# Scoring part of the edges of a graph attention layer with edges on partitions

## The chip, the cores and the metric

The kernel runs on one core of one Trainium2 chip. The metric is the device time of one execution in microseconds (us); the figure given is the median of several runs. The engines named here are TensorE (PE in the profile; its weight loads are shown as PEld), VectorE (DVE), ScalarE (ACT), GpSimd (POOL) and the queue that issues the transfers (SP).

## The reference, cut to what matters

Four graph layers, each with a layer norm and a relu ahead of it and a residual sum behind it, work on x of shape 128 x 64 x 256 (batches, nodes, features). The change touches the fourth layer only, a graph attention with 4 heads of 64 features over 512 edges. Its input H is the normed x; A0 is the adjacency matrix; src and dst are the two ends of each edge.

```python
Xq = (H @ W_lin.T).reshape(bt, n, h, dh)
Xv = (H @ W_val.T).reshape(bt, n, h, dh)
Qs = Xq[:, src]
Kt = Xq[:, dst]
e = jnp.einsum('behd,hd->beh', jax.nn.leaky_relu(Qs + Kt, LRELU_SLOPE), a)
e = e + jnp.log(A0[src, dst] + EPS)[None, :, None]
e_t = e.transpose(1, 0, 2)
m = jax.ops.segment_max(e_t, src, num_segments=n)
ex = jnp.exp(e_t - m[src])
denom = jax.ops.segment_sum(ex, src, num_segments=n)
attn = ex / denom[src]
Vt = Xv[:, dst].transpose(1, 0, 2, 3)
Y = jax.ops.segment_sum(attn[..., None] * Vt, src, num_segments=n)
return Y @ W_out.T
```

LRELU_SLOPE is 0.2, so leaky_relu(z) is 0.2 z + 0.8 relu(z). The 0.2 part is linear in Xq and is formed per node; the 0.8 relu part has to be formed per edge. It is the second part that the change forms in another way.

## The kernel before, in words

All arithmetic is float32. Nearly all instructions are recorded under line 799 of the kernel, a helper which every operation goes through, so the profile is read by the names of tiles.

The fourth layer (`layer3`, from line 2416) works through 32 steps g = 0..31. A step holds 4 of the 128 batches. The 32 steps form 4 groups of 8 steps, and a group's scores are collected in one PSUM tile acc of 128 x 512: 32 batches x 4 heads on partitions, the 512 edges in columns. The steps of a group go through these functions:

- `turned` (line 2471, in even steps): the layer norm of the next block of 8 batches (tile h, pool with two slots), its transposes (h to ps, copied to hT) and the sums hS which the next function needs.
- `queries` (line 2501, in odd steps): seven products, from which Q (the Xq of 8 batches, nodes on partitions) and XV (their Xv) are put together by additions on VectorE. Then `linear` (2535): Q times 0.2 a (tile lin_p), reduced to lin by two reductions, the linear part of the score per node.
- `score` (2550): for each of two halves fc of the features and each of the 4 batches k, one matmul of 64 rows: weights are Q (64 nodes x 128 features), the moving operand is S2, which holds a one for each end of each edge (64 nodes x 512 edges). Even and odd k use partitions 0 to 63 and 64 to 127. The result ps (128 features x 512 edges) goes through a relu on ScalarE into r (8 slots). So a step has eight score matmuls and eight relus, ps with features on partitions.
- `reduce` (2563): eight matmuls add r into acc, with weights from apad, which holds 0.8 a in the columns of the step's batches and heads (64 columns wide; even k go to the upper, odd k to the lower half of acc). The first step of a group writes the logarithm of A0 into acc.
- `summed` (2643, at the end of a group): one matmul adds the linear part, lin times S2. Then `softmax` with `shifted` (2631, 2647): scans along the edges on VectorE over acc, the exponential on ScalarE; `edgewise` (2659), a group later: the transposes of the result into at.
- For step v = g - 10, ten steps behind: `between` (2671) multiplies at by the one-hot OST (tiles aw, 5 slots, four products of 128 x 1024 on VectorE per step) and gathers them by matmuls with ODT (ps, then an); `weighted` (2698) multiplies an with XV into y; `output` (2714) multiplies y with W_out, adds the result to X on VectorE and sends X to HBM.
- The first eight steps also bring back blocks of X that had been put aside (`back`, line 2227: transposes of ls_t into ps, added to X by VectorE).
- `turn` (2576) finishes the last group and the steps which are still open, in an order written out by hand.

The ps tiles of all these functions share five PSUM slots; acc and y have one place each. Outside `turn` the order on each engine is made when the kernel is built, from the order in the program and from when operands are expected to be ready; within an engine the instructions then stand in that order. So a function which stands late in the program can be placed into an earlier gap of its engine.

Of the kernel before, what the change touches and what calls it, by code (L numbers as in the profile page):

```python
# [8 lines left out]
F32 = mybir.dt.float32  # L9
I32 = mybir.dt.int32  # L10
AF = mybir.ActivationFunctionType
ALU = mybir.AluOpType
# [63 lines left out]
class Eig:  # L76
# [12 lines left out]
    def t(self, name, *shape, dt=F32):  # L89
        key = (name, shape)  # L90
        if key not in self.tiles:
            n = "e_" + name + "_" + "_".join(map(str, shape))
            self.tiles[key] = self.pool.tile([64, *shape], dt, name=n)
        return self.tiles[key]
# [748 lines left out]
class Plan:  # L843
# [56 lines left out]
    def rest(self):  # L900

        while any(self.queue.values()):
            for e in self.queue:
                self.fill(e, 1e9)
# [8 lines left out]
class Fast:  # L913
# [229 lines left out]
    def scale(self):  # L1143
# [32 lines left out]

        Q = t("Q", 64, 2, 64)
        o.ts(Q[:, 0, :], D[:], mid[:], ALU.subtract, sc[:], ALU.mult)
        nes = self.NE = t("NEs", 64, 64)
        o.ts(nes[:], NE[:], sc[:], ALU.mult)  # L1180
        o.stt(Q[:, 1, :], nes[:], -1.0, nes[:], ALU.mult, ALU.mult)
        self.ne2 = Q[:, 1, :]
        p = self.mm((self.k.ones[0:1, :], Q[0:1, :, :].rearrange("p a b -> p (a b)")), p=128, n=128)
        DD, E2 = self.DD, self.E2 = t("DD", 128, 64), self.ME[:, 1, :]
# [258 lines left out]
B, N, D = 128, 64, 256  # L1443
P = 128
NB = 16
TPB = 4
BT = 512
E = 512
HEADS = 4
# [16 lines left out]
class Kernel:  # L1466
# [949 lines left out]
    def layer3(self):  # L2416
        nc, o, io = self.nc, self.o, self.io
        cx, (w,) = self.stage([("l3x", 1)], "tile")
        with cx:
            cy, pools = self.stage([("l3", 2), ("l3v", 2), ("l3s", 1), ("l3r", 6), ("l3ps", 5), ("l3cps", 1), ("l3yps", 1)], "tile")  # L2420
            with cy:
                self.a02 = self.everywhere(w, "ed_a", io["L3_gnn_a"].rearrange("h d -> (h d)"))
                o.ts(self.a02[:], self.a02[:], 0.2, ALU.mult)
                self.drop, self.dropr = (w.tile([P, E], F32, name="ed_" + n) for n in ("drop", "dropr"))
                o.ts(self.drop[:], self.cont[:], 1.0, ALU.subtract, FLOOR, ALU.mult)
                o.ts(self.dropr[:], self.contr[:], 1.0, ALU.subtract, FLOOR, ALU.mult)
                WQV = w.tile([P, 2, 2 * D], F32, name="w3_qv")
                for x, n in enumerate(("W_lin", "W_val")):
                    nc.sync.dma_start(WQV[:, :, x * D:(x + 1) * D],
                                      io[f"L3_gnn_{n}_t"].rearrange("(k p) m -> p k m", p=P))  # L2430
                WO = self.weights(w, "w3_o", io["L3_gnn_W_out_t"])


                st, LAG = {}, 10
                self.turned(st, 0, *pools)
                WQV = self.sums3(w, WQV)
                self.queries(st, 0, WQV, *pools)()
                for g in range(8 * NG):
                    v = g - LAG
                    ahead = (g + 1) // 2 if g % 2 and g + 1 < 8 * NG else None  # L2440
                    self.score(st, g, *pools)
                    if v >= 1:
                        self.weighted(st, v - 1, *pools)
                    self.reduce(st, g, *pools)
                    if g % 8 == 1 and 1 < g:
                        self.edgewise(st, g // 8 - 1, *pools)
                    if v >= 0:
                        self.between(st, v, *pools)
                    if g % 8 == 7 and g + 1 < 8 * NG:
                        self.summed(st, g // 8, *pools)  # L2450
                    if g < 8:
                        self.back(8 + g, pools[4], "ps")
                    if ahead:
                        rest = self.queries(st, ahead, WQV, *pools)
                    elif g + 2 < 8 * NG:
                        self.turned(st, g // 2 + 1, *pools)
                    if g + 6 == 8 * NG:

                        p = pools[4].tile([P, BT], F32, name="ps")
                        for c in range(4):  # L2460
                            self.nc.tensor.transpose(p[:N, c * P:(c + 1) * P], self.OST[:, c, :], self.ident[:])
                        self.act_copy(self.cont[:N, :], p[:N, :])
                    if v >= 1 and g + 1 < 8 * NG:
                        self.output(st, v - 1, WO, *pools)
                    if ahead:
                        rest()
                    if g % 8 == 7 and g + 1 < 8 * NG:
                        self.softmax(st, g // 8, *pools)
                self.turn(st, WO, pools)
# [31 lines left out]
    def queries(self, st, i, WQV, pool, vp, sp, rp, psum, psc, psy):  # L2501

        nc, o, (A, S1, S2, S3) = self.nc, self.o, st["sums", i]
        Q = st["Q", i] = rp.tile([P, TPB, D], F32, name="Q", bufs=1)
        V = st["V", i] = rp.tile([P, TPB, D], F32, name="XV", bufs=7)
# [29 lines left out]
    def linear(self, st, i, pool, vp, sp, rp, psum, psc, psy):  # L2535

        o, Q = self.o, st["Q", i]

        if i % 4 == 0:
            st["lin", i // 4] = pool.tile([P, 2, 2, 8, HEADS], F32, name="lin")  # L2540
            self.nc.vector.memset(st["lin", i // 4][:], 0.0)
        lin, pr = st["lin", i // 4], sp.tile([P, TPB, D], F32, name="lin_p")
        o.mul(pr[:], Q[:], self.a02[:, None, :].to_broadcast([P, TPB, D]))
        k = 2 * (i % 4)
        for x in range(2):
            s = slice(64 * x, 64 * x + 64)
            o.red(lin[s, x, :, k:k + 2, :].rearrange("p m a h -> p a m h"),
                  pr[s].rearrange("p (a m) (h d) -> p a m h d", m=2, h=HEADS), ALU.add)

    def score(self, st, g, pool, vp, sp, rp, psum, psc, psy):  # L2550

        rs = st["r"] = []
        Q = st["Q", g // 2]
        for fc in range(2):
            for k in range(4):
                s = slice(64 * (k % 2), 64 * (k % 2) + 64)
                p = psum.tile([P, E], F32, name="ps")
                self.mm(p[:], Q[s, 2 * (g % 2) + k // 2, fc * P:(fc + 1) * P], self.S2[s, :])
                r = rp.tile([P, E], F32, name="r", bufs=8)
                self.act(r[:], p[:], AF.Relu)  # L2560
                rs.append(r)

    def reduce(self, st, g, pool, vp, sp, rp, psum, psc, psy):


        q, i = g // 8, g % 8
        if i == 0:
            st["acc", q] = psc.tile([P, E], F32, name="acc")
            self.mm(st["acc", q][:], self.ones[0:1, :], self.logA[:], True, False)
        for fc in range(2):  # L2570
            for k in range(4):
                z = 64 - 32 * (k // 2) - 4 * i
                x = 64 * (k % 2)
                self.mm(st["acc", q][x:x + 64, :], self.apad[:, fc, z:z + 64], st["r"][4 * fc + k][:], False, False)

    def turn(self, st, WO, pools):

# [64 lines left out]

    def summed(self, st, q, pool, vp, sp, rp, psum, psc, psy):

        self.mm(st["acc", q][:], st["lin", q][:].rearrange("p x m a h -> p (x m a h)"), self.S2[:], False, True)

    def shifted(self, st, q, pool, vp, sp, rp, psum, psc, psy):
# [144 lines left out]
```

## Time and profile before

| what | value |
| --- | --- |
| median of 3 runs | 2331.29 us (2325.34 to 2333.49) |
| the profiled execution | 2327.79 us |
| its span, from first to last instruction | 2326.0 us |
| fourth layer in that span | about 1746 to 2322.6 us |
| granted TensorE clock, mean | 0.997 |

Times in the profile are microseconds from the start of the span, unless marked ns. "out<-in" names the tiles that an instruction writes and reads; "128*64" behind a matmul is the part of the array it uses, rows by columns; "128x512" is partitions by elements; "x16" counts records, and one matmul call in float32 leaves two records, each with its weight load. The busy time of an engine counts stretches in which at least one of its instructions runs, so for matmuls that run beside each other it is less than count times mean. In a timeline the bracket behind an instruction is the time for which its engine had stood idle ahead of it, and what ended that.

### The profile page before, as it was taken

To read this page: it belongs to the slowest core of one execution; us is meant where nothing else is said; L and a number is where in the kernel's file an instruction comes from. 1 tells how busy PE (TensorE), PEld (TensorE's weight loads), DVE (VectorE), ACT (ScalarE), POOL (GpSimd) and SP (SyncE) were. 2 spreads that over 40 slices of the span, in tenths; PEclk is the share of its full clock that TensorE was granted. 3 is DMA by queue.
4 is the path that set the end of the run, shared out by engine and by line. 5 is a ranking of instruction groups with operands and counts; after the bars stand their busy time and mean duration, and the time that the engine had idled before them with its cause. 6 is when DMAs were issued, how large, how long until landed. Compare 5 with 4: busy or idle time off the path is not lost.

```text
span 2326.0 us, 33145 instructions
## 1 busy us (share of the span) xinstructions
PE 2283.2 (98%) x12365; PEld 1664.8 (72%) x12365; DVE 1642.2 (71%) x4073; ACT 1129.4 (49%) x2468; POOL 3.0 (0%) x26
## 2 busy tenths in 40 slices
PE   7999998999999999999999999999999999999999
PEld 4555446986777788888999998888885544554544
DVE  7887676998447777666766666559756686766667
ACT  5666864654436654443444444336435544444321
POOL 0000000000000000000000000000000000000000
PEclk9999999999999999999999999999999999999999
DMA  5000221230010000001000002000010000000001
GB/s 172 1 2 22 66 59 32 69 83 19 1 37 1 1 19 1 1 1 37 1 1 1 1 1 73 1 1 17 1 47 26 1 5 15 14 19 14 15 24 46
DMA packets 61210, 54.89 MB, mean 24 GB/s; under 512 B 15219, under 2 KB 58868, under 8 KB 61044
## 3 DMA queue, kind: packets, MB, share of 16 engines
q1 hardware_dynamic: 61044, 52.73, 7.5%
q8 instruction: 98, 1.61, 0.3%
q14 instruction: 68, 0.56, 0.1%
HBM read 35.93 MB, written 16.78 MB: 23 GB/s over the span
## 4 chain that ended last, share of the span: by engine, by line
PE 80%; DVE 3%; issue 1%; ACT 0%; ACTq 0%; DVEq 0%
PE ps L799 69%; PE acc L799 5%; PE pt L799 4%; PE pe L799 1%; PE y L799 1%; DVE X L799 1%; DVE aw L799 1%; DVE sm_m L799 0%; DVE XV L799 0%; ACT ls_g L799 0%; DVE ls_g L799 0%; DVE ls_t L799 0%; DVE sm_e L799 0%; DVE lin L799 0%; DVE Q L799 0%
## 5 line engine op out<-in xcount | busy, mean ns | idle before, releaser
L799 ACT ACTIVATE ls_g<-ls_g,ls_b 128x512 f32<-128x512 f32 (+4 forms) x472 | 243.1, 565 | 152.0 <-DVE ls_g L799 150.2
L799 ACT ACTIVATE ls_g<-ps,ls_b 128x256 f32<-128x256 f32 (+3 forms) x268 | 115.6, 471 | 330.6 <-PE ps L799 327.3
L799 PE MATMUL ps<-z,w 128*128 128x512 f32 x512 | 255.3, 622 | 0.9 <-ACT z L799 0.9
L799 PE MATMUL ps<-big,X 128*128 128x176 f32 (+3 forms) x848 | 212.9, 366 | 0.8 <-ACT big L799 0.7
L799 DVE TENSOR_TENSOR ls_g<-ls_z,ps 128x512 f32<-128x512 f32 (+5 forms) x256 | 146.9, 579 | 91.6 <-PE ps L799 90.0
L799 DVE TENSOR_TENSOR aw<-at,ed_OST 128x1024 f32<-128x1024 f32 x128 | 149.9, 1219 | 83.0 <-PE ps L799 82.8
L799 PE MATMUL ps<-ls_tx,X 128*128 128x160 f32 (+2 forms) x960 | 206.9, 326 | 0.6 <-ACT ls_g L799 0.6
L799 PE MATMUL ps<-X,X 128*128 128x160 f32 (+1 forms) x896 | 199.1, 306 | 0.0
L799 PE MATMUL ps<-X,ls_w 128*128 128x256 f32 x640 | 190.4, 379 | 0.0
L799 PEld LDWEIGHTS ps<-ls_tx,X 128*128 128x128 f32 x960 | 161.8, 190 | 15.2 <-DVE X L799 4.9
L799 PEld LDWEIGHTS ps<-big,X 128*128 128x128 f32 x848 | 145.9, 190 | 30.6 <-issue 19.4
L799 DVE TENSOR_TENSOR X<-ls_g 128x1024 f32<-128x1024 f32 (+2 forms) x108 | 117.4, 1087 | 49.9 <-ACT ls_g L799 49.9
L799 ACT ACTIVATE r<-ps 128x512 f32<-128x512 f32 x256 | 131.7, 615 | 41.5 <-PE ps L799 41.4
L799 PEld LDWEIGHTS ps<-X,X 128*128 128x128 f32 x896 | 148.4, 190 | 0.0
L799 PE MATMUL ps<-X,ls_s 128*128 128x256 f32 x480 | 142.3, 379 | 0.0
L799 PEld LDWEIGHTS ps<-z,w 128*128 128x128 f32 x512 | 87.6, 190 | 69.8 <-issue 61.4
L799 PE MATMUL ps<-ls_tx,ls_s 128*128 128x256 f32 x464 | 134.7, 379 | 0.0
L799 PE MATMUL ps<-ed_S,Q 64*128 64x512 f32 x512 | 132.8, 618 | 1.4 <-DVE hT L799 0.7
L799 PEld LDWEIGHTS ps<-X,ls_w 128*128 128x128 f32 x640 | 121.4, 190 | 16.8 <-DVE X L799 0.3
L799 PE MATMUL ps<-ls_tx,ls_w 128*128 128x256 f32 x464 | 133.2, 380 | 0.0
L799 PE MATMUL ps<-big,ls_w 128*128 128x256 f32 x464 | 131.8, 379 | 0.7 <-ACT ls_z L799 0.7
L799 ACT ACTIVATE h<-X,n_m,n_r 128x256 f32<-128x256 f32 x192 | 101.4, 589 | 40.9 <-issue 25.0
(557 smaller groups left out, 4087.6 us busy)
## 6 DMA issues: line engine op xcount, KB each, us to landing
X<-in_x_dram SPq DMA_DIRECT2D x32, 512.0 KB
xs<-X SPq DMA_DIRECT2D x16, 512.0 KB
X<-xs SPq DMA_DIRECT2D x16, 512.0 KB
out_dram<-X SPq DMA_DIRECT2D x31, 256.0 KB
X<-in_L_gnn_Wih_t_dram SPq DMA_DIRECT2D x4, 512.0 KB
ls_w<-in_L_gnn_Wih_t_dram SPq DMA_DIRECT2D x4, 512.0 KB
ls_w<-in_L_gnn_Whh_t_dram SPq DMA_DIRECT2D x4, 512.0 KB
w<-in_L_gnn_W_t_dram SPq DMA_DIRECT2D x2, 512.0 KB
```

The costliest lines, as they stand in the source:

```text
L799: i = method(*a, **kw)
```

## The change

In 14 of the 32 steps (steps 2, 4 and 6 of groups 0 to 2, and steps 2 to 6 of group 3, by `BY_EDGES`) two of the four batches of a step are scored in another way. For these two batches the roles of the operands are exchanged: the weights are 128 edges of S2, the moving operand is the batch's Q (64 nodes x 256 features), and the result has edges on partitions and features in columns. Eight matmuls of 64 rows and 256 columns take the place of four of 64 rows and 512 columns. Their four results of 128 x 512 go through the relu on ScalarE as before. The sum over features, for these two batches, is no longer made by `reduce` on TensorE but by the new function `heads` on VectorE: a product with 4 x 0.2 a, and a reduction over the 64 features of each head into a new tile by (edges on partitions, 4 x 128). GpSimd sets by to zero at the first step of each group. `heads` stands at the end of a step in the program, ahead of the softmax. `summed` adds by to acc by four more matmuls per group, which transpose it.

Two smaller edits: r has 10 slots instead of 8, and lin_p is taken from the pool and under the name of h, whose two slots it now shares.

```diff
                     if ahead:
                         rest()
+                    self.heads(st, g, *pools)
                     if g % 8 == 7 and g + 1 < 8 * NG:
                         self.softmax(st, g // 8, *pools)
...
-        lin, pr = st["lin", i // 4], sp.tile([P, TPB, D], F32, name="lin_p")
+        lin, pr = st["lin", i // 4], pool.tile([P, TPB, D], F32, name="h")
...
-        rs = st["r"] = []
+
+        nc, mine = self.nc, g % 8 in self.BY_EDGES[g // 8]
         Q = st["Q", g // 2]
+        st["r"], st["rows"] = {}, []
+        rows = lambda x: slice(64 * x, 64 * x + 64)
         for fc in range(2):
-            for k in range(4):
-                s = slice(64 * (k % 2), 64 * (k % 2) + 64)
+            for k in range(2 if mine else 4):
+                s = rows(k % 2)
                 p = psum.tile([P, E], F32, name="ps")
                 self.mm(p[:], Q[s, 2 * (g % 2) + k // 2, fc * P:(fc + 1) * P], self.S2[s, :])
-                r = rp.tile([P, E], F32, name="r", bufs=8)
+                r = st["r"][fc, k] = rp.tile([P, E], F32, name="r", bufs=10)
                 self.act(r[:], p[:], AF.Relu)
-                rs.append(r)
+        for c in (0, 2) if mine else ():
+            ps = [psum.tile([P, 2, D], F32, name="ps") for x in range(2)]
+            for k in range(2):
+                for x in range(2):
+                    self.mm(ps[x][:, k, :], self.S2[rows(x), (c + k) * P:(c + k + 1) * P],
+                            Q[rows(x), 2 * (g % 2) + 1, :])
+            for x in range(2):
+                r = rp.tile([P, E], F32, name="r", bufs=10)[:].rearrange("p (c d) -> p c d", c=2)
+                self.act(r, ps[x][:], AF.Relu)
+                st["rows"].append((r, c, x))
...
             self.mm(st["acc", q][:], self.ones[0:1, :], self.logA[:], True, False)
-        for fc in range(2):
-            for k in range(4):
-                z = 64 - 32 * (k // 2) - 4 * i
-                x = 64 * (k % 2)
-                self.mm(st["acc", q][x:x + 64, :], self.apad[:, fc, z:z + 64], st["r"][4 * fc + k][:], False, False)
+            st["by", q] = vp.tile([P, 4, P], F32, name="by", bufs=1)
+            self.nc.gpsimd.memset(st["by", q][:], 0.0)
+        for fc, k in st["r"]:
+            z = 64 - 32 * (k // 2) - 4 * i
+            x = 64 * (k % 2)
+            self.mm(st["acc", q][x:x + 64, :], self.apad[:, fc, z:z + 64], st["r"][fc, k][:], False, False)
+
+
+    BY_EDGES = (2, 4, 6), (2, 4, 6), (2, 4, 6), (2, 3, 4, 5, 6)
+
+    def heads(self, st, g, pool, vp, sp, rp, psum, psc, psy):
+
+        o, by = self.o, st["by", g // 8]
+        for r, c, x in st["rows"]:
+            o.stt(r, r, 4.0, self.a02[:, None, :].to_broadcast([P, 2, D]), ALU.mult, ALU.mult)
+            z = 64 * x + 32 + 4 * (g % 8)
+            o.red(by[:, c:c + 2, z:z + HEADS], r.rearrange("p c (h d) -> p c h d", h=HEADS), ALU.add)
...
     def summed(self, st, q, pool, vp, sp, rp, psum, psc, psy):
 
+        for c in range(4):
+            self.mm(st["acc", q][:, c * P:(c + 1) * P], st["by", q][:, c, :], self.ident[:], False, False)
         self.mm(st["acc", q][:], st["lin", q][:].rearrange("p x m a h -> p (x m a h)"), self.S2[:], False, True)
```

## The prediction

> **What bounds the kernel now.** I read the busy shares by slices first, then the stretch of the fourth layer, which is all that the change touches.
>
> ```profile
> PE 2283.2 (98%) x12365; PEld 1664.8 (72%) x12365; DVE 1642.2 (71%) x4073; ACT 1129.4 (49%) x2468; POOL 3.0 (0%) x26
> PE   7999998999999999999999999999999999999999
> DVE  7887676998447777666766666559756686766667
> ```
>
> TensorE (PE) is the only engine at 98%, and the last ten slices, the fourth layer, are nines for it and fives to eights for VectorE (DVE). The busy time by stretches says it in numbers. The columns are the stretch and its length, then busy us of PE, weight loads, DVE and ACT: a steady pair of steps, the stretch from the reduction of step 26 to that of step 31, and the whole layer.
>
> ```profile
> 1934.90:1968.60 33.70, 33.70 (x216) 17.59 (x212) 21.86 (x37) 13.69 (x30) 0.00 (x0) 1.00 0.05 17
> 2163.40:2244.70 81.30, 81.30 (x521) 41.61 (x516) 45.97 (x56) 28.53 (x58) 0.00 (x0) 1.00 0.05 17
> 1746.00:2322.60 576.60, 573.04 (x3496) 299.19 (x3494) 396.20 (x607) 236.11 (x462) 0.00 (x0) 0.99 0.05 17
> ```
>
> PE idles 3.6 of 576.6 us there, DVE 180. So a microsecond of PE work removed is a microsecond won, for as long as DVE, ACT and the five PSUM slots keep up. What a step is made of stands in PE's timeline (start, length, instruction), here from the score of the even step 20 to the score of step 21:
>
> ```profile
> 2054.39 3.91 PE L799 MATMUL ps<-ed_S,Q 64*128 64x512 f32 x16
> 2058.23 0.69 PE L799 MATMUL y<-an,XV 64*64 64x64 f32 x32
> 2058.86 3.65 PE L799 MATMUL acc<-r,ed_apad 128*64 128x512 f32 x16
> 2062.34 3.60 PE L799 MATMUL ps<-aw,ed_ODT 128*64 128x512 f32 x16
> 2065.88 1.09 PE L799 MATMUL ps<-ident,h 128*128 128x128 f32 x8
> 2066.80 1.89 PE L799 MATMUL ps<-w_o,y 128*128 128x256 f32 x8
> 2068.63 3.97 PE L799 MATMUL ps<-ed_S,Q 64*128 64x512 f32 x16
> ```
>
> Each call of a matmul is two records (eight score calls a step, x16). Taken from start to start, acc costs 3.48 us, the score 3.84, eight passes over 256 columns 1.83 and eight over 128 columns 0.92. One 64-row score pass lasts 618 ns by its group's mean, yet sixteen fit in 3.84 us: passes on the two halves of the rows run beside each other.
>
> DVE's timeline in the same steps shows the room for new work (in brackets: idle time before it, and what ended it):
>
> ```profile
> 2053.64 0.69 DVE L799 TENSOR_TENSOR Q<-XV,ps 128x512 f32<-128x512 f32 x1 [1.04 <-PE ps L799]
> 2058.99 0.42 DVE L799 COPY y<-y 128x256 f32<-128x256 f32 x1 [0.39 <-PE y L799]
> 2064.26 3.50 DVE L799 TENSOR_TENSOR aw<-at,ed_OST 128x1024 f32<-128x1024 f32 x3 [4.84 <-PE ps L799]
> 2067.67 0.68 DVE L799 COPY hT<-ps 128x512 f32<-128x512 f32 x1
> 2069.74 0.68 DVE L799 TENSOR_TENSOR X<-X,ps 128x512 f32<-128x512 f32 x1
> ```
>
> From step 12 on DVE stands still for 4.84 us before aw in nearly every step (in the first group, 3.9 or less before the X adds), until PE has read the old aw tiles: just behind the eight relus, where the new work becomes ready.
>
> **The change, part by part.**
>
> *Score.* In a changed step four of eight score calls go, half of 3.84, 1.92 us. In their place come eight calls of 64 rows and 256 columns, sixteen passes. No row has this form. A full-array pass over 256 columns (w_t, eight from 2047.39 to 2049.12) takes 0.216 us; beside each other in halves that is 0.108 each, 1.73 for sixteen. From below: 1.73, a gain of 0.19 a step. From above: no overlap, 3.46, a loss of 1.54 a step, or 21.6 us in all. Between them I take an exchange at nothing, since the nearest form, the score itself, overlaps, and the short y passes (64 columns, 32 in 0.63 us) do too. The two halves write two different slots, as now.
>
> On this one page speaks against the change: the Trainium skill's "TensorEngine Tiling (Array Packing)", section Instruction Overhead, gives each matmul an overhead of about 60 cycles and advises against cutting short what is already short. With the 2.4 GHz of "TensorE: Matmul & The Clock Gate" (specification table) that is an estimate of 25 ns a pass; eight passes more than before, in two halves, would be 0.1 us a step, 1.4 us in all. The rows show less: twice 0.216 for 256 columns against 0.435 for a pair of 512-column acc passes (3.48 / 8).
>
> *Reduce.* Four of eight acc calls go: half of 3.48, 1.74 us a step, on the path; 14 steps give **24.4 us**. The four that stay read relus that are done first, so they wait for no later relu.
>
> *Summed.* Four calls of 128 columns are added per group, eight passes, for four groups 32 passes. The transposes of h take 0.115 each (eight in 0.92), the few of sm_e 2.6 us for 16, 0.163 each: 3.7 to 5.2. I take the first row, being back to back as these are, rounded up: **4 us**, on the path (softmax waits for acc, PE is full).
>
> *Relus.* Eight of 128x512 per step before and after: nothing.
>
> *Heads.* Four scalar_tensor_tensor and four tensor_reduce a step on DVE. Both have rows, although the new reduce writes eight results where this one writes one:
>
> ```profile
> L799 DVE TENSOR_REDUCE ed_rank<-ed_cmp 128x1 f32<-128x512 f32 x4 | 2.7, 665 | 0.1
> ...
> L799 DVE SCALAR_TENSOR_TENSOR sm_m<-ed_contr,sm_m 128x512 f32<-128x512 f32 x3 | 2.1, 686 | 0.0
> ```
>
> By these means a step costs 4 x (0.686 + 0.665) = 5.4 us; back to back, where the timeline shows starts 0.60 apart for 128x512 (X to hT, 2069.74 to 2070.34), 4.8. From below 4.8, from above the 128x1024 rows, 1.22 each, 9.8. I take 4.8, the repeated operand costing lin_p nothing (1225 ns for 1024, as aw). All 14: 67 us of DVE time, against 180 idle less some 20 that PE saves. Cover: the 4.84 us gap, which shrinks with acc to 3.1. Heads wait for the last relus (ACT is through with them at about 2059.6); behind them stand the copy of y, whose reader on PE comes 7 us later, and aw, read a whole step later. The reader of by comes a step after the last heads: over 10 us in hand. The remaining 1.7 pushes aw, hT and X, not past their old moments by much but against a PE that comes 1.74 earlier.
>
> *What is late next.* Steps 10, 12, 14, 18, 20, 22, 26, 28, 30: the next score wants slots, and hT and X are still in two of them. With those evacuated at their old times, I set the score's four pairs by hand: two free slots at once, the third pair only after the hT copy and two relus, the end 0.5 later than wished. So 0 to 0.5 a step; I take 0.3, nine times, 2.7. Steps 2, 4, 6 (no gather, but two X adds of the fetched block in slots as well; the odd score there already takes 4.9): 0 to 1.74, I take 0.8, 2.4. Steps 27 and 29: aw, then XV and Q of the next queries follow directly on heads, and Q has 1.04 idle ahead of it: 0 to 1.74, I take 1.1, 2.2. Together **7.3 us**.
>
> *The rest.* lin_p moves to the two slots of h: h for the next block is written only after the transposes of the last (ACT's h at 2067.50, transposes from 2065.88), and lin_p lives 4 us in the other slot: nothing; if the cover goes, h waits at most those 4 us once a pair, with a pair's time in hand. r has ten slots: the seventh relu of the next step needs the first one freed by heads, about 2061, and comes at about 2071: 10 us in hand. The zeroing of by on GpSimd has 0.2 us rows at 128x128, and its first reader comes two steps later: nothing. DMAs keep their place, only the X add ahead of each output moves, and the output's landing is waited for only at the very end.
>
> **Sum.** 24.4 - 4 - 7.3 = 13.1 us less, against the profiled execution: 2327.79 (span 2326.0 and 1.8 around it) becomes 2314.7. That execution lies 3.5 under the median 2331.29; the same 13.1 from the median gives 2318.
>
> **Rivals.**
>
> *VectorE saturates in the last group only.* From 2163.4 to 2244.7 DVE is busy 45.97; five heads make it 70 to 73, and PE needs 81.3 - 8.7 = 72.6. A queue so full can hold PE in each of these five steps. If they win nothing, and the other nine lose the upper end of their waits (six times 0.5, three times 1.74), the sum is 15.7 - 4 - 8.2 = 3.5 less: 2328, no change that can be told. For it: the numbers stand level. Against it: DVE's order fills gaps already (hT stands between two aw).
>
> *The new VectorE forms are slow.* The decisive point is (72.6 - 46.0) / 5 = 5.3 us a step in the last group; elsewhere a pair allows 32.0 - 21.9 = 10.1. Each further microsecond costs 5 there. At the upper end, 9.8 a step, that is 22.5: 22.5 - 13.1 = 9.4 slower, 2341. Even is at about 7.9 a step, 1 us an instruction. Against it: three rows of this size lie at 0.6 to 0.7.
>
> *The halves do not run beside each other at 256 columns.* 21.6 - 13.1 = 8.5 slower: 2340; even at 0.94 lost a step. For it: the only short 64-row form without a partner, ed_contr, takes 1.2 us for 8 passes. Against: y.
>
> **Chances.** The forecast's case 0.66, with another 0.03 for the waits all at zero and a shorter score (24.4 + 2.7 - 3.7, 23.4 less, 2308). Saturation of the last group 0.15. Slow VectorE forms 0.09, no overlap 0.07. A twenty-fifth of the forecast's own case falls inside 0.3% (7 us, about what a measurement of this kernel can tell from no change): faster 0.67, same 0.17, slower 0.16. The range runs from 2308 (all unknown costs at the lower end) to 2333, which takes in the first rival and the runs' own scatter; the two slow cases, 0.16, stay out.
>
> **What would show it.** acc passes with r 400 instead of 512, each pair still 0.43; 64-row passes over 256 columns, sixteen in about 1.75 us (3.5 means no overlap); reduce and product on DVE at 0.66 to 0.69 and their place in the gap before aw; even steps shorter by 1.2 to 1.7; DVE at 82% of the layer ((396 + 67) / 563); PE idle under 10 us. Wrong it would be if PE waits for Q or XV for over a microsecond in each of steps 10 to 30, or if the relu or hT waits of the score grow beyond 1 us a step.

## The result, and the profile after

The changed kernel takes 2356.56 us (median of 4 runs, 2354.31 to 2359.94) against 2328.32 for the kernel before in runs beside it (2325.26 to 2333.49): a ratio of 1.0117, 95% interval 1.0103 to 1.0132. The forecast was 13.1 us faster; the kernel became 28 us slower. The profiled execution took 2356.01 us, its span 2354.2.

The page of the changed kernel, with the three lines that the prediction showed of the kernel before:

```profile
PE 2295.0 (97%) x12397; PEld 1679.2 (71%) x12397; DVE 1709.7 (73%) x4185; ACT 1134.6 (48%) x2468; POOL 5.1 (0%) x30
PE   7999998999999999999999999999999999999999
DVE  7877676998447777766777667569656786877887
```

PE is busy 11.8 us more, although it was given some 20 us less to do. The nines of PE are where they were: by these digits nothing is wrong. VectorE has the 67.5 us that it was to have.

Busy time by stretches (length, then PE, weight loads, DVE, ACT; PEclk is the granted clock) of the changed kernel: steps 20 and 21, then the layer from its first score matmul to the end:

```profile
2083.48:2118.19 34.71, 33.73 (x214) 18.34 (x213) 26.23 (x43) 14.15 (x28) 0.00 (x0) 1.00 0.05 16
1759.39:2354.20 594.81, 572.64 (x3503) 306.14 (x3502) 459.90 (x723) 241.37 (x464) 1.57 (x3) 0.98 0.05 15
```

and the same two stretches of the kernel before:

```profile
2054.39:2088.14 33.75, 33.75 (x214) 17.62 (x213) 20.77 (x30) 13.55 (x27) 0.00 (x0) 1.00 0.05 17
1756.32:2326.00 569.68, 564.35 (x3471) 292.58 (x3470) 389.53 (x587) 232.19 (x457) 0.00 (x0) 1.00 0.05 16
```

The layer is 25.1 us longer, and 3.1 us of the 28.2 between the two profiles lie ahead of it, in a part that the change does not edit; over the fourteen profiles of this study the layer's first score begins between 1752.8 and 1762.6. So what follows is attributed by the length of the layer, and each kernel's verdict goes by its median.

Where the 25.1 come from: acc passes less, 14 steps by 1.71, is -23.9; the new passes of `summed`, about +3.8; PE idle 22.2 in place of 5.3, +16.9; PE at half clock for 17.1 us (shown below), by an estimate half of that, +8.5. (In the last of these windows sixteen acc passes, 4.4 us of them at half clock, take 5.66 in place of 3.48; where PE waits for slots, a window may cost less.) That leaves 19.8 us which PE's rows call busy. They are in the score: summed over the 32 steps, PE is busy there for 153.7 us in place of 131.6. PE's timeline of the changed kernel from step 20 to the score of step 21, to be held against the one in the prediction:

```profile
2083.48 1.99 PE L799 MATMUL ps<-ed_S,Q 64*128 64x512 f32 x8
2085.30 1.66 PE L799 MATMUL ps<-Q,ed_S 64*128 64x256 f32 x10
2087.23 1.13 PE L799 MATMUL ps<-Q,ed_S 64*128 64x256 f32 x6 [0.28 <-ACT r L799]
2088.29 0.69 PE L799 MATMUL y<-an,XV 64*64 64x64 f32 x32
2088.92 1.94 PE L799 MATMUL acc<-r,ed_apad 128*64 128x512 f32 x8
...
2096.97 2.99 PE L799 MATMUL ps<-ed_S,Q 64*128 64x512 f32 x10
2100.67 1.98 PE L799 MATMUL ps<-ed_S,Q 64*128 64x512 f32 x6 [0.71 <-DVE X L799]
```

From start to start acc takes 1.76, as forecast. But the changed score takes 4.81 (2083.48 to 2088.29) in place of 3.84, waiting for relus, and the score of the next, unchanged step 5.61 (to 2102.58) in place of 3.90, waiting for X. ScalarE's timeline shows the first of the two:

```profile
2082.35 1.08 ACT L799 ACTIVATE h<-X,n_m,n_r 128x256 f32<-128x256 f32 x2
2084.64 0.60 ACT L799 ACTIVATE r<-ps 128x512 f32<-128x512 f32 x1 [1.21 <-PE ps L799]
2085.13 0.59 ACT L799 ACTIVATE h<-X,n_m,n_r 128x256 f32<-128x256 f32 x1
2085.62 0.59 ACT L799 ACTIVATE r<-ps 128x512 f32<-128x512 f32 x1
2086.10 0.59 ACT L799 ACTIVATE h<-X,n_m,n_r 128x256 f32<-128x256 f32 x1
2086.59 2.06 ACT L799 ACTIVATE r<-ps 128x512 f32<-128x512 f32 x4
2089.35 0.20 ACT L799 ACTIVATE n_y<-n_v 128x4 f32<-128x4 f32 x1 [0.71 <-DVE n_v L799]
```

Two of norm's four h stand among the relus, 0.49 us each, though ScalarE had idled 1.21 us just before. Before the change all four stood in its idle time, ahead of the score of the odd step, as ScalarE's timeline of the kernel before has it:

```profile
2055.55 4.03 ACT L799 ACTIVATE r<-ps 128x512 f32<-128x512 f32 x8 [2.18 <-PE ps L799]
...
2067.50 2.06 ACT L799 ACTIVATE h<-X,n_m,n_r 128x256 f32<-128x256 f32 x4
```

In the changed kernel, ahead of the seventh relu, ScalarE also waits for VectorE's n_v, to take a square root for norm. VectorE's timeline of the changed kernel shows the second:

```profile
2087.72 0.18 DVE L799 RECIPROCAL n_r<-n_y 128x4 f32<-128x4 f32 x1
...
2089.15 0.17 DVE L799 TENSOR_SCALAR n_v<-n_mv 128x4 f32<-128x4 f32 x1
2089.23 1.29 DVE L799 SCALAR_TENSOR_TENSOR r<-r,ed_a 128x512 f32<-128x512 f32 x2
...
2094.46 3.48 DVE L799 TENSOR_TENSOR aw<-at,ed_OST 128x1024 f32<-128x1024 f32 x3
2097.87 0.68 DVE L799 COPY hT<-ps 128x512 f32<-128x512 f32 x1
...
2099.94 0.68 DVE L799 TENSOR_TENSOR X<-X,ps 128x512 f32<-128x512 f32 x1
```

Norm's small instructions (1.5 us from 2087.72) stand in front of the new work, this in front of aw, and hT and X behind them all; they hold two of the five PSUM slots, and the score of step 21 had begun at 2096.97. In the kernel before they stood behind X, which had begun at 2069.74:

```profile
2070.68 0.17 DVE L799 RECIPROCAL n_r<-n_y 128x4 f32<-128x4 f32 x1
```

So the change moved norm, on both engines. The one edit that touches norm is the shared slots of lin_p and h. Why norm is placed there when the two share slots stays open.

Group 0 shows a third thing. VectorE's timeline there:

```profile
1847.70 0.68 DVE L799 SCALAR_TENSOR_TENSOR r<-r,ed_a 128x512 f32<-128x512 f32 x1
...
1851.73 6.01 DVE L799 TENSOR_REDUCE by<-r 128x8 f32<-128x512 f32 x10
1857.66 1.28 DVE L799 SCALAR_TENSOR_TENSOR r<-r,ed_a 128x512 f32<-128x512 f32 x2
```

Ten reductions stand in a row in step 7, those of steps 2 and 4 (whose products ran from 1790 on) among them; until then their r slots stay taken, and steps 5 to 7 of group 0 lose 13.4 us between them. And three times PE's clock is halved after a stop (stretches as above; the 0.50 ahead of the last two columns is the clock):

```profile
1844.50:1847.90 3.40, 3.40 (x14) 1.87 (x11) 0.81 (x2) 1.09 (x2) 0.00 (x0) 0.50 0.00 0
1854.70:1861.50 6.80, 6.80 (x15) 2.52 (x16) 5.43 (x10) 3.72 (x7) 0.00 (x0) 0.50 0.00 0
1953.70:1960.50 6.80, 6.80 (x46) 2.28 (x46) 0.42 (x1) 2.06 (x4) 0.00 (x0) 0.50 0.07 23
```

### The profile page after: what moved, and what is told of

Its sections match the earlier page's. It is cut to its first block, busy times and chain, and to the rows that moved or that the text cites. A ratio compares the mean times of both kernels' runs of the same rounds, so it can differ in the third digit from the quotient of the medians.

```text
span 2354.2 us, 33360 instructions
## 1 busy us (share of the span) xinstructions
PE 2295.0 (97%) x12397; PEld 1679.2 (71%) x12397; DVE 1709.7 (73%) x4185; ACT 1134.6 (48%) x2468; POOL 5.1 (0%) x30
## 4 chain that ended last, share of the span: by engine, by line
PE 73%; DVE 10%; issue 1%; ACT 1%; DMA 0%; DVEq 0%; ACTq 0%
PE ps L799 64%; PE pt L799 4%; PE acc L799 3%; DVE aw L799 2%; DVE r L799 1%; DVE lin L799 1%; PE pe L799 1%; DVE by L799 1%; DVE X L799 1%; PE y L799 1%; DVE h L799 1%; DVE XV L799 0%; DVE hT L799 0%; DVE n_st L799 0%; DVE n_r L799 0%
## 5 line engine op out<-in xcount | busy, mean ns | idle before, releaser
L799 PE MATMUL ps<-ed_S,Q 64*128 64x512 f32 x400 | 117.8, 628 | 13.2 <-DVE X L799 5.7
```

Source lines behind the costliest of these rows:

```text
L799: i = method(*a, **kw)
```

## The experiments

The theories. A: the shared slots move norm's h among the relus, and that is a main part of the loss. B, the rival and the prediction's view: the sharing costs nothing. C: the late reductions of group 0 cost its steps 5 to 8; its rival D: those steps are slow whatever the reductions do. Later E, that the new work delays hT and X, and F, that the sharing costs by moving norm as a whole.

The twelve kernels run, with the two of the case on top. "Layer" is as above, from the profile of one execution, where the median is of several; "half" is the time at half clock in it, without the last 4 us of the span.

| kernel | median us | ratio to before, 95% interval | layer | PE idle in it | half |
| --- | --- | --- | --- | --- | --- |
| before | 2328.32 | | 569.7 | 5.3 | 0 |
| changed | 2356.56 | 1.0117 (1.0103 to 1.0132) | 594.8 | 22.2 | 17.1 |
| share_only | 2341.13 | 1.0046 (1.0033 to 1.0059) | 582.8 | 7.5 | 3.4 |
| held_h | 2334.39 | 1.0014 (1.0005 to 1.0024) | 571.2 | 8.0 | 0 |
| by_w | 2351.31 | 1.0089 (1.0076 to 1.0102) | 589.6 | 20.5 | 17.1 |
| by_w_r8 | 2350.78 | 1.0089 (1.0075 to 1.0102) | 591.3 | 20.8 | 20.5 |
| by_w_lin | 2322.86 | 0.9962 (0.9948 to 0.9976) | 560.8 | 10.4 | 0 |
| last_w_lin | 2327.99 | 0.9989 (0.9980 to 0.9998) | 567.0 | 6.2 | 0 |
| after_h_first | 2349.13 | 1.0085 (1.0073 to 1.0097) | 589.2 | 27.8 | 10.2 |
| share_h_first | 2344.04 | 1.0061 (1.0048 to 1.0074) | 589.8 | 26.4 | 23.9 |
| norm_late | 2318.76 | 0.9955 (0.9942 to 0.9969) | 559.8 | 9.9 | 0 |
| lin_noheads | 2310.10 | 0.9916 (0.9903 to 0.9930) | 548.5 | 4.6 | 0 |
| late_aw | 2309.83 | 0.9923 (0.9910 to 0.9936) | 551.6 | 7.7 | 0 |
| h_first_late | 2331.16 | 0.9999 (0.9990 to 1.0008) | 567.6 | 18.3 | 6.8 |

### The sharing alone (share_only)

```diff
-        lin, pr = st["lin", i // 4], sp.tile([P, TPB, D], F32, name="lin_p")
+        lin, pr = st["lin", i // 4], pool.tile([P, TPB, D], F32, name="h")
```

> The kernel before, with one edit of the change alone: lin_p takes the two slots of h. Theory A (the sharing is a main part of the loss: norm's four h relus of the next block may no longer run early in ScalarE's idle time, because the slots of one name are given out in program order): 4 to 8 us slower than before, 2332 to 2336, with h written after lin_p in each pair of steps. Theory B (the sharing costs nothing by itself, as the prediction said): within 0.1% of before, 2326 to 2331.

Measured: 2341.13 against 2330.82, slower by 0.46%; the layer is 13.1 us longer. More than theory A wanted, and B falls. Most even steps from 8 to 28 take 0.97 more (twice 0.49), the others about half of that, 8.9 us in all. Steps 9 and 17 take 3.1 and 1.5 more and step 11 takes 1.0 less: steps 9 and 17 follow a softmax, and norm's small instructions, behind hT before, now stand on VectorE between its last product and hT, for which PE stands 2.33 us in step 9 (0.74 before). Steps 0 to 7 lose next to nothing in sum: there the h stood among the relus of the odd steps before, and now do in the even ones. PE's timeline of step 20's score in this kernel:

```profile
2062.63 4.88 PE L799 MATMUL ps<-ed_S,Q 64*128 64x512 f32 x16
```

Sixteen passes, no bracket, no idle time: PE is "busy" for 4.81 us (to the next start, 2067.44) with what took 3.84. By the single records the passes on the two halves no longer start together: the last four come one by one, each about half a microsecond behind the one before, as a slot comes free.

### h in the same late place, but ahead of the relus (held_h)

```diff
+        f = self.factors(pool, *self.moments(pool, i))
+        self.nc.hold((None, None, st.get("behind")))
-        h = self.norm(pool, i)
+        h = self.norm(pool, i, by=f)
+        self.nc.hold()
...
                         rest()
+                        st["behind"] = self.nc.mark()[2]
```

> The kernel before, lin_p in its own place, with norm's h held on ScalarE behind the copy into Q of the last queries, so that h is written a step later than before, at the place where the sharing puts it. In this order the four h stand side by side ahead of the first relu of an even step's score, or three of them, where the sharing leaves two of the four among the relus. Theory A, made sharper (each h that stands among the relus of a score holds that score up by one h, 0.49 us; the place as such costs nothing, because ScalarE idles 2.2 us ahead of the first relu): as before, 2326 to 2333. The rival (h is written too late, and what reads it comes late): as with the sharing, 2338 to 2343.

Measured: 2334.39 against 2329.41, 0.14% slower; the layer is 1.5 us longer, not 13.1. In ten of the fourteen even steps that hold them the four h stand in ScalarE's idle time; of these, steps 12, 14, 18, 20 and 22 take 0.06 longer or less (0.97 with the sharing). What is lost is in steps 8, 9 and 17 (0.5, 1.5 and 2.0), and steps 0 to 7 and 11 win 2.9. So in the even steps it is standing among the relus that costs, and not the late place; in steps 9 and 17 the late place does cost, 3.5 of the 4.6 that they lose with the sharing, and in step 9 norm's small instructions again stand ahead of hT, with a stop of 2.45 us. In this kernel VectorE has none of the new work.

### by in a pool of its own (by_w)

```diff
-            st["by", q] = vp.tile([P, 4, P], F32, name="by", bufs=1)
-            self.nc.gpsimd.memset(st["by", q][:], 0.0)
+            st["by", q] = self.by
+            if q:
+                self.nc.gpsimd.memset(self.by[:], 0.0)
...
+                self.by = w.tile([P, 4, P], F32, name="by")
+                nc.vector.memset(self.by[:], 0.0)
```

> The changed kernel with by in a pool of its own that lives for the whole layer, zeroed once at the layer's start for group 0 (GpSimd zeroes it for the later groups). The reductions of group 0 then stand directly behind their products, two or three at a time, where in the changed kernel twelve stand in a row in step 7. Theory C (group 0 loses its time because r slots stay held until step 7): steps 5 to 8 come back to their old lengths, 10 to 14 us less than the changed kernel, 2342 to 2347. Theory D (those steps are slow because of the half clock and of ScalarE's pace, whatever the reductions do): under 4 us less, 2353 or more.

Measured: 2351.31, and the layer 5.2 us shorter than the changed kernel's. The reductions stand directly behind their products now, but steps 5 to 7 come only part of the way: they take 46.1 us, against 55.4 in the changed kernel and 42.0 before, and step 3 loses 2.5. Theory C had the size wrong by a half; the sharing holds these steps too, as the next kernel shows (42.2). What puts the reductions late when by comes from the other pool was not found.

### lin_p in its own place as well (by_w_lin), and the number of r slots alone (by_w_r8)

```diff
-        lin, pr = st["lin", i // 4], pool.tile([P, TPB, D], F32, name="h")
+        lin, pr = st["lin", i // 4], sp.tile([P, TPB, D], F32, name="lin_p")
...
-                r = st["r"][fc, k] = rp.tile([P, E], F32, name="r", bufs=10)
+                r = st["r"][fc, k] = rp.tile([P, E], F32, name="r", bufs=8)
...
-                r = rp.tile([P, E], F32, name="r", bufs=10)[:].rearrange("p (c d) -> p c d", c=2)
+                r = rp.tile([P, E], F32, name="r", bufs=8)[:].rearrange("p (c d) -> p c d", c=2)
```

> As the last, and lin_p has its own place again, with 8 r slots in place of 10 to make room. If theory A holds (sharing costs 4 to 8): 2334 to 2342. If theory B holds: as the last or some us slower, since two r slots are gone. If what remains is the new VectorE work ahead of hT and X, this kernel stays above the kernel before in groups 1 and 2.

The second has only the lines on r:

> The changed kernel with by in a pool of its own and lin_p still in h's slots, but 8 r slots. The kernel with lin_p in its own place differed from the one with by in its own pool by two edits, the place of lin_p and 8 in place of 10 r slots; this one separates them. If the place of lin_p is the whole difference of 28 us: 2349 to 2354. If fewer r slots give a better order: 2345 or less.

Measured: 2322.86 with lin_p in its own place, faster than the kernel before by 0.38%; 2350.78 with 8 r slots alone, no different from 10. So lin_p's place is worth 28 us, and all 14 changed steps were still there. The layers differ by 28.8 (589.6 to 560.8), twice the sharing alone: 13.7 in the even steps, about as there, and 15.1 in the odd ones, 13.6 of these in steps 3, 7, 13 and 15, where the clock was halved for 17 us.

This kernel is the change as the prediction had reckoned it. Twelve of the 14 changed steps are 1.71 shorter than before; steps 27 and 29, whose own scores wait for the X of the step ahead of them, are 0.9 and 0.5 shorter. The changed score takes 3.84, of which the sixteen short passes are 2.02. ScalarE's order is that of the kernel before, and what is late is X:

```profile
2054.82 4.03 ACT L799 ACTIVATE r<-ps 128x512 f32<-128x512 f32 x8 [2.18 <-PE ps L799]
...
2065.06 2.06 ACT L799 ACTIVATE h<-X,n_m,n_r 128x256 f32<-128x256 f32 x4
```

```profile
2066.19 2.94 PE L799 MATMUL ps<-ed_S,Q 64*128 64x512 f32 x10
2069.35 1.98 PE L799 MATMUL ps<-ed_S,Q 64*128 64x512 f32 x6 [0.23 <-DVE X L799]
```

```profile
2066.55 0.68 DVE L799 COPY hT<-ps 128x512 f32<-128x512 f32 x1
...
2068.62 0.68 DVE L799 TENSOR_TENSOR X<-X,ps 128x512 f32<-128x512 f32 x1
```

The first fence is ScalarE in steps 20 and 21, the third VectorE, and the second PE in the score of step 21, which takes 5.07 us for 3.90: 0.23 shown as idle, the rest passes without a partner.

### The last group alone (last_w_lin)

```diff
-    BY_EDGES = (2, 4, 6), (2, 4, 6), (2, 4, 6), (2, 3, 4, 5, 6)
+    BY_EDGES = (), (), (), (2, 3, 4, 5, 6)
```

> As the last, with the changed steps in the last group alone (five of 32). In the traces the stretch of steps 26 to 30 took 5.6 us less after the change than before. Theory A and C together: nothing else costs, so 4 to 6 us less than the kernel before, 2322 to 2325. The rival of the prediction (five heads saturate VectorE in the last group): 2328 or more.

Measured: 2327.99 against 2330.82, faster by 0.11% (0.02 to 0.20), less than expected; the layer is 2.7 us shorter. Steps 26 to 30 take 6.6 less, but `summed` adds 0.9 to 1.0 in each group (steps 7, 15, 23) though by is zero there, and step 31 with the turn 1.98. VectorE does not saturate in the last group: the rival falls.

### ScalarE's order mended under the sharing (after_h_first, share_h_first)

```diff
+                st["h"] = self.norm(pools[0], 1)
+                st["first"] = nc.mark()[2]
...
                         rest()
+                        if ahead + 1 < 4 * NG:
+                            st["h"] = self.norm(pools[0], ahead + 1)
+                            st["first"] = nc.mark()[2]
...
-        h = self.norm(pool, i)
+        h = st.pop("h", None) or self.norm(pool, i)
...
+                nc.hold((None, None, st.pop("first", None)))
                 self.act(r[:], p[:], AF.Relu)
+                nc.hold()
```

The first is the changed kernel with these lines, the second has by in its own pool besides.

> The changed kernel, sharing and by as they are, with ScalarE's order alone mended: norm of the next block is called behind the queries, and the first relu of the next score is held behind its four h, so that none of them stands among the relus. Theory A as the whole of what the sharing costs: the 28 us that lin_p's own place brought come back without it, 2325 to 2332 (the late reductions of group 0 stay). If the sharing also costs by its two slots, lin_p or h waiting for the other: 2338 or more.

> The same order of ScalarE, with by in a pool of its own as well. Theory A: like the kernel with lin_p in its own place, 2319 to 2326. If the two shared slots cost by themselves: 2332 or more.

Both missed: 2349.13 and 2344.04. The layer of the second is as long as by_w's (589.8, 589.6); its median is 7 us lower, and in its profile the layer begins 7.2 earlier. Theory A as the whole of the cost falls. The changed scores are nearly all back at their old lengths (step 6 of the first takes 7.67), but the odd scores got worse by as much: step 21's takes 6.58 in the second. ScalarE and then VectorE in the second kernel:

```profile
2072.45 2.06 ACT L799 ACTIVATE h<-X,n_m,n_r 128x256 f32<-128x256 f32 x4
2074.74 3.06 ACT L799 ACTIVATE r<-ps 128x512 f32<-128x512 f32 x6 [0.22 <-PE ps L799]
2079.45 0.21 ACT L799 ACTIVATE n_y<-n_v 128x4 f32<-128x4 f32 x1 [1.65 <-DVE n_v L799]
2079.56 1.07 ACT L799 ACTIVATE r<-ps 128x512 f32<-128x512 f32 x2
```

```profile
2077.82 0.18 DVE L799 RECIPROCAL n_r<-n_y 128x4 f32<-128x4 f32 x1
...
2079.33 1.29 DVE L799 SCALAR_TENSOR_TENSOR r<-r,ed_a 128x512 f32<-128x512 f32 x2
...
2087.97 0.68 DVE L799 COPY hT<-ps 128x512 f32<-128x512 f32 x1
```

The relus were ready early; norm's small instructions for the block after next still stand in front of the new work (1.5 us from 2077.82), and ScalarE waits 1.65 for n_v with two relus left. This gave theory F.

### Norm's small instructions behind the last aw (norm_late)

```diff
                         if ahead + 1 < 4 * NG:
-                            st["h"] = self.norm(pools[0], ahead + 1)
+                            nc.hold((None, st.get("worked"), None))
+                            f = self.factors(pools[0], *self.moments(pools[0], ahead + 1))
+                            nc.hold()
+                            st["h"] = self.norm(pools[0], ahead + 1, by=f)
...
                         self.between(st, v, *pools)
+                        st["worked"] = nc.mark()[1]
...
                     self.heads(st, g, *pools)
+                    if g % 2 == 0 and g < 10:
+                        st["worked"] = nc.mark()[1]
```

> As the kernel with by in its own pool, lin_p sharing h's slots and the four h ahead of the first relu; and the small instructions of norm for the block after that (bn_stats, the n_ tiles, about 2 us on VectorE, and the square root that ScalarE takes between two relus) are held on VectorE behind the last aw product, so that the new work starts as early as where lin_p has its own place. Theory F (the sharing costs by moving norm as a whole: its h among the relus, its small instructions in front of the new work and so in front of hT and X): 2320 to 2328, as with lin_p in its own place. If the shared slots cost something apart from norm's place: 2335 or more.

Measured: 2318.76 against 2328.17, ratio 0.9955, a little under the range that theory F gave. The layer takes 559.8 us, lin_p's own place 560.8. With the sharing still there, its cost goes when norm's place on the two engines is mended. Theory F stands. The order is not quite that of by_w_lin (seven odd steps are 0.6 to 0.7 shorter, steps 8 and 27 are 1.0 and four others up to 0.4 longer), so a cost of the shared slots by themselves of some 3 us is not excluded.

### Without the new VectorE work (lin_noheads)

The kernel with by and lin_p in their own places, without the call of `heads`; by stays zero, so half of the score of the changed steps is left out.

```diff
-                    self.heads(st, g, *pools)
```

> The kernel with by and lin_p in places of their own, without the new products and reductions on VectorE, so that by stays zero and half of the score of the changed steps is left out. TensorE and ScalarE have the same work. Theory E (the odd step behind a changed step loses up to 1.2 us because VectorE comes to hT and X late, behind the new work): 7 to 10 us less than with it, 2313 to 2316. The prediction's view (TensorE itself arrives earlier at evacuations that keep their old times): at most 3 us less, 2320 or more.

Measured: 2310.10, 12.8 less than with it, more than theory E wanted; the layer is 12.3 shorter. All odd scores are back at their old lengths. So the VectorE work, at the forecast duration, costs 12.3 us of the path, and the 3 us of the expectation's second view fall. The picture behind that view does not: with the work hT and X of step 20 begin 12.89 and 14.96 us behind the start of its score (2053.66), against 13.28 and 15.35 before, so nearly at their old moments, while PE's step is 1.71 shorter. Without the work they begin at 11.57 and 13.64, as early as PE, which waits for nothing (4.6 us idle in the layer). It is the work that holds them at their old moments.

### The aw products behind X (late_aw, h_first_late)

```diff
-        self.gathered(st, g, (self.spread(st, g, c, *pools) for c in (0, 2)), *pools)
+        late = st.pop("late", None)
+
+        def spread(c):
+            self.nc.hold((None, late if c else None, None))
+            W = self.spread(st, g, c, *pools)
+            self.nc.hold()
+            return W
+
+        self.gathered(st, g, (spread(c) for c in (0, 2)), *pools)
...
                         self.output(st, v - 1, WO, *pools)
+                        if g % 2 == 0 and g % 8 in self.BY_EDGES[g // 8]:
+                            st["late"] = nc.mark()[1]
```

> The kernel with by and lin_p in places of their own, and in the step behind a changed even step the later two of the four aw products are held on VectorE behind the X addition, which frees a PSUM slot for the score. Theory E: the score of the odd steps loses its 1.2 us no longer, 4 to 7 us less, 2316 to 2319. If the gathers then wait for the aw products, or the slots are not what the score waits for: 2322 or more.

Measured: 2309.83 against 2329.41, ratio 0.9923 (0.9910 to 0.9936): the fastest of the kernels that form the whole score, and faster than both kernels of the case. 13.0 less than the kernel it is built on by medians, 9.2 in the layer; the odd steps behind a changed one get back 1.24 each from step 13 on (0.81 in step 27), which is all that they had lost. Step 11 gets back nothing: step 10 has no X addition. Its timelines, VectorE and then PE's score of step 21, at its old 3.84:

```profile
2056.46 1.21 DVE L799 TENSOR_TENSOR aw<-at,ed_OST 128x1024 f32<-128x1024 f32 x1
2057.66 0.69 DVE L799 COPY hT<-ps 128x512 f32<-128x512 f32 x1
...
2059.82 0.69 DVE L799 TENSOR_TENSOR X<-X,ps 128x512 f32<-128x512 f32 x1
2060.43 3.49 DVE L799 TENSOR_TENSOR aw<-at,ed_OST 128x1024 f32<-128x1024 f32 x3
```

```profile
2059.72 3.91 PE L799 MATMUL ps<-ed_S,Q 64*128 64x512 f32 x16
```

X is done at 2060.51, 0.8 us into the score, instead of 3.1 us into it. The same edit on share_h_first:

> As the last, and the later two aw products behind a changed even step held behind the X addition, which took 13 us where lin_p had its own place (about 9 of it inside the fourth layer). Same effect here: 9 to 13 us less than the last, 2308 to 2315. If the two edits want the same idle time of VectorE: under 4 us less.

Measured: 2331.16, 12.9 less than share_h_first, inside the 9 to 13 expected but above 2315, and level with the kernel before. The profiled layers differ by more, 22.2, of which up to 8.5 is less half clock. Holding aw back mends much of what the sharing had done to hT and X, and not all.

## Why the prediction was wrong, point by point

- **The failed step** is the sentence on lin_p: "h for the next block is written only after the transposes of the last ..., and lin_p lives 4 us in the other slot: nothing; if the cover goes, h waits at most those 4 us once a pair, with a pair's time in hand". It asked who would wait for h. Nobody does. But norm moved into the changed step: its h among the relus, its small instructions ahead of the new work. That costs 28.8 us of the layer, up to 8.5 of them by the half clock, and 13.1 even without the rest of the change (share_only, by_w_lin, norm_late). From kernel to kernel the 25.1 us of the layer are 28.8 for lin_p's place, 5.2 for by's, 12.3 for the new VectorE work, and 21.2 won by the rest (lin_noheads against before), for which the forecast had 24.4 - 4 = 20.4. With lin_p and by in their own places the time falls inside the forecast's range (2322.9 measured, 2318 forecast, range 2308 to 2333), and the layer is 8.9 shorter than before where 13.1 was forecast; the rest is the term of what is late next, below.
- **r and by**: "10 us in hand" for r, "nothing" for the zeroing. In group 0 the first reduction came 61 us after its product (1790.6 to 1851.7), and r was held as long. Giving by its own pool brought 5.2 us of the layer (by_w). The number of slots did not matter with by there (by_w_r8).
- **Reduce**: 1.74 a step forecast, 1.71 measured in all 14 steps of by_w_lin (from start to start acc takes 3.48 before and 1.77 there in most steps).
- **Score**, exchanged at nothing: right where nothing is moved (3.84 before, 3.84 in by_w_lin), wrong in the changed kernel (4.81), by the relus. Passes of 256 columns do run beside each other: sixteen in 2.02 us, and in 1.93 in share_h_first, so rival three falls. The estimate from the Trainium skill's "TensorEngine Tiling (Array Packing)", Instruction Overhead, 0.1 us a step, cannot be told from zero here: the two figures differ by as much. The same page's section PSUM Bottleneck bears on what did happen: packing speeds up TensorE but not the emptying of PSUM, which may become the bottleneck (after a fourfold speedup, the page says; here it is two halves). This trace agrees: in the changed kernel the score of step 20 takes 4.81 us for 3.84, waiting for relus, and the next 5.61 for 3.90, waiting for X.
- **Summed**: 4 us forecast; the group of 32 is busy 4.6, and 0.9 to 1.0 a group is measured (last_w_lin), some 3.8 in all.
- **Heads**: 0.686 and 0.665 forecast, from these two groups of the changed kernel 0.682 and 0.676, so the second rival falls:

```profile
L799 DVE SCALAR_TENSOR_TENSOR r<-r,ed_a 128x512 f32<-128x512 f32 x56 | 36.8, 682 | 2.9 <-ACT r L799 2.8
L799 DVE TENSOR_REDUCE by<-r 128x8 f32<-128x512 f32 x56 | 36.1, 676 | 0.3
```

- **What is late next**: the right place and mechanism, mis-sized. 7.3 us forecast; 12.3 measured in by_w_lin (lin_noheads is that much shorter). That hT and X would be "not past their old moments by much" came true: in by_w_lin they are 0.39 ahead of them, and PE is 1.71 ahead. What was mis-sized is what so late an X costs the next score, set by hand in pairs of passes and taken at 0.3. X is done 3.1 us into that score, 1.8 before, and most of the loss is passes without a partner: nine even steps from 10 on cost 10.8 in the step that follows, not 2.7 (1.84 in step 11, 0.8 in 27, else 1.1 to 1.2). Steps 2, 4 and 6, forecast 0.8 each, cost 0.5. The 1.1 each for Q and XV behind steps 27 and 29 did not show: the scores of steps 28 and 30 take 3.84, as before.
- **The last group** does not saturate: steps 26 to 30 gain 5.6 even in the changed kernel.
- The forecast's own warnings came true ("the relu or hT waits of the score grow beyond 1 us a step", PE idle above 10), by another cause than it named.
- The half clock was in no term. By the estimate above it is up to 8.5 of the 25.1 us.

## What to carry to other kernels

Giving a tile another tile's slots is a change of order: look at every producer of both names, on every engine, and ask what it will now stand in front of, not only who waits for the data. When matmuls run in pairs on two halves of the array, a full PE row is no proof of full speed; time the group from start to start. Where one engine's work frees PSUM for another, look at what stands in front of it: here, holding two products behind one addition was worth 9 us of a 561 us layer.

## What was not expected of the hardware

- PE's clock was halved for 3.4, 6.8 or 10.2 us at a time. In the layer, from its first score on and without the last 4 us, all of the 21 such windows but one begin within 1.8 us of the end of a PE stop of 0.9 to 2.3 us; the one, in by_w_r8 at 2157.8, has no stop of over 0.3 us in the 50 us ahead of it. Kernels with under 11 us of PE idle in the layer had none, apart from share_only, with one. The Trainium skill's "TensorE: Matmul & The Clock Gate", Part 1 (The HAM clock gate), has activity judged over windows of about 3.4 us, and the half clock after an idle window. The lengths here agree, but no stop was as long as 3.4 us, and the measurement decides. Neither is there a plain threshold: a stop of 2.33 us in the changed kernel (at 1884.9) and one of 2.45 in held_h were followed by no such window. That the stops cause the windows was not tried by itself, and stays open.
- An engine that takes 0.49 us a relu can unpair PE's passes: two foreign instructions on ScalarE, 0.97 us together, cost PE 0.97 us without a nanosecond of idle time in its row.
